# Transforms along w on quarters of the array, and a second spectral layer in groups of 192 channels

## The chip, the cores and the metric

The kernel runs on one core of a Trainium2 chip. The metric is the device time of one execution in microseconds (us), measured beside other executions of the same program; the median of three is given. One further execution was taken with the hardware profiler, and all rows shown are of that one. The engines are named as in the profile: PE is TensorE's matmul, PEld its weight load, DVE is VectorE, ACT is ScalarE, POOL is GpSimd, SP is SyncE, which issues most DMAs.

## The reference

Four layers run one after the other on an image of 48 x 48 positions with 768 channels, all in fp32. Layer 0 is an attention block with an MLP, layer 2 a scan of twelve steps with a 3x3 convolution. Layers 1 and 3 are the spectral layers, and they are what the change is about:

```python
bias = x
xs = jnp.fft.rfft2(xf32, axes=(1, 2))                     # along h and w, 48 x 25 modes
xs = xs.reshape(B, H, Wm, NUM_HEADS, BLOCK)               # 8 blocks of 96 channels
o1r = relu(einsum(xr, w1[0]) - einsum(xi, w1[1]) + b1[0]) # complex two-layer MLP per block
o1i = relu(einsum(xi, w1[0]) + einsum(xr, w1[1]) + b1[1])
o2r = einsum(o1r, w2[0]) - einsum(o1i, w2[1]) + b2[0]
o2i = einsum(o1i, w2[0]) + einsum(o1r, w2[1]) + b2[1]
out_c = softshrink(zr, LAMBDA) + 1j * softshrink(zi, LAMBDA)
out = jnp.fft.irfft2(out_c, s=(H, W), axes=(1, 2))
return out + bias
```

The transforms are linear, so the residual `bias` can be added to the image after the way back, or to the spectrum along w before the last step back.

## The kernel before

The transform over the image is done as matmuls with small constant matrices, in two steps: along w (48 positions to 25 modes with a real and an imaginary part) and along h.

*Forward along w, `spectrum_rows` (L1493).* A block is one of six groups `g` of eight image rows, and one `half` of the channels (384). The tile x has 96 partitions, two image rows side by side, and four such pairs. Four matmuls with a block-diagonal matrix `fw2` of 96 x 112 (two copies of the 48 to 50 transform, interleaved) each stream 384 columns (L1501). `Evac` copies the four results in turn on ACT and DVE to `ys`, and one DMA on SP stores it to `yu[half]` in DRAM, which has 112 rows, 24 pairs of image rows and 384 channels.

In the first spectral layer these blocks are called by `afno_follow` (L1642) from the MLP phase, where they stand among the MLP's matmuls: the MLP's second layer (L1029) stores a part of the image, `follow` loads it as `f1_x`, and a later call does the block. Their PSUM places come from the MLP's pool `ml_t` of two places (L909), which the transposes of the MLP use too; the MLP's products use another pool, `ml_m`, of six. The last of the twelve blocks is done at the start of `afno_first`. In the second spectral layer `rows_in` calls them between the matmuls of the scan's output (L1371), whose results get their bias on DVE (L1373), into a temporary tile, and Silu on ACT (L1374), into `x3`, a tile that holds the whole image with 96 partitions.

*The items, `spectrum_mix` (L1536).* For each half of the channels and each of five groups `kc` of five modes, the spectrum is loaded (`f_yt`, L1530), and four items, one for each block of 96 channels, are worked: transform along h (`f_x`, L1565), MLP (L1579 to L1581, L1600, L1601), softshrink on DVE, and back along h (`f_u`, L1615). The 40 items of a layer run as a pipeline of four stages. The result `f_us` goes back to `yu`. In the first layer (`keep` true) DVE adds the result to the loaded spectrum (L1618), so that the residual is in the spectrum; in the second layer `Evac` only copies.

*Back along w.* In the first layer `back` in `afno_first` (L1697) has the spectrum `f_gt` stationary (L1702). In the second layer `back` in `afno_second` (L1792 to L1804) takes a block of `yu` that is loaded ahead (`f_gt`, L1790, 100 of 112 rows used), does four matmuls with the block-diagonal `iw` of 100 x 96 (L1798), adds the result to `x3` on DVE (L1800), and issues the store on ACT's queue. The six blocks of the first half of the channels stand among the items of the second half; the six of the second half come behind all items, and their loads wait for the stores of the last items. For these the rows of the first four `kc` are loaded ahead (`most`) and the remaining rows last (`rest`).

A scheduler of the language orders the instructions of each engine from their dependences, and places of a pool are given out in turn. [...]

## Time and profile before

| what | value |
|---|---|
| median of three runs | 3671.11 us (3670.99 to 3674.01) |
| profiled execution, its own time | 3666.73 us |
| its span, first to last instruction | 3664.9 us |
| mean granted TensorE clock | 0.987 |
| MLP phase, with the first layer's rows in it | about 1660 to 2685 us |
| items of the first spectral layer | about 2685 to 2872 us |
| scan output with the second layer's rows | about 3320 to 3428 us |
| items of the second spectral layer | about 3428 to 3634 us |

Columns of the groups: line, engine, operation, out<-in, partitions x columns of the array with the shape, count, then busy time in us and mean ns of one, then idle time of the engine before them and what ended it. A record of a matmul lasts longer than its share of the array, as matmuls are pipelined; what counts is the time from one start to the next. Columns of the stretches: from and to, length, busy time (and count) of PE, PEld, DVE, ACT and POOL, granted TensorE clock, share of the DMA engines, GB/s. Columns of the timeline: start, duration, engine, line, operation, out<-in, shape, count of merged instructions, and in brackets idle time before.

### The profile page before, as it was taken

To read this page: it belongs to the slowest core of one execution; us is meant where nothing else is said; L and a number is where in the kernel's file an instruction comes from. 1 tells how busy PE (TensorE), PEld (TensorE's weight loads), DVE (VectorE), ACT (ScalarE), POOL (GpSimd) and SP (SyncE) were. 2 spreads that over 40 slices of the span, in tenths; PEclk is the share of its full clock that TensorE was granted. 3 is DMA by queue.
4 is the path that set the end of the run, shared out by engine and by line. 5 is a ranking of instruction groups with operands and counts; after the bars stand their busy time and mean duration, and the time that the engine had idled before them with its cause. 6 is when DMAs were issued, how large, how long until landed. Compare 5 with 4: busy or idle time off the path is not lost.

```text
span 3664.9 us, 52305 instructions
## 1 busy us (share of the span) xinstructions
PE 3567.0 (97%) x20914; PEld 2157.0 (59%) x20914; DVE 1998.1 (55%) x3011; ACT 1138.9 (31%) x1731; POOL 702.3 (19%) x570
## 2 busy tenths in 40 slices
PE   7999989999999999999999999999999998999998
PEld 4666544444444444455555555555578867995685
DVE  6644356667666666655324323332345578994455
ACT  1222244444444444303201210121023365223341
POOL 4211101111111111151000000000023303971131
PEclk9999989999999999999999999999999999999999
DMA  7666665646454443344345333533444302113345
GB/s 256 227 223 202 205 198 151 180 139 165 134 144 134 117 122 105 97 136 158 102 129 177 119 106 122 166 106 109 152 131 112 99 20 103 36 30 85 101 119 155
DMA packets 267739, 491.83 MB, mean 134 GB/s; under 512 B 37182, under 2 KB 220286, under 8 KB 261280
## 3 DMA queue, kind: packets, MB, share of 16 engines
q1 hardware_dynamic: 257680, 467.45, 42.9%
q10 hardware_dynamic: 9808, 20.94, 1.6%
q8 instruction: 168, 2.75, 0.3%
q14 instruction: 83, 0.68, 0.1%
HBM read 344.69 MB, written 143.62 MB: 133 GB/s over the span
## 4 chain that ended last, share of the span: by engine, by line
PE 82%; DMA 2%; DVE 2%; ACT 1%; issue 1%; POOL 1%; SPq 0%; DVEq 0%; ACTq 0%; POOLq 0%
PE p L966 13%; PE p L1029 13%; PE s L629 12%; PE av L660 12%; PE c L1286 6%; PE c L1193 4%; PE s L639 3%; PE pj L169 2%; PE f_z L1600 2%; PE f_z L1601 2%; PE f_x L1565 2%; PE so L1371 2%; PE f_u L1615 2%; PE f_w L1798 1%; PE f_o L1579 1%; PE f_o L1580 1%
## 5 line engine op out<-in xcount | busy, mean ns | idle before, releaser
L649 DVE TENSOR_TENSOR acc<-acc,p 128x928 f32<-128x928 f32 (+1 forms) x480 | 567.9, 1183 | 253.3 <-ACT p L641 220.6
L641 ACT ACTIVATE p<-s 128x928 f32<-128x928 f32 (+1 forms) x540 | 506.1, 939 | 524.4 <-PE s L639 496.3
L629 PE MATMUL s<-qt,kv 64*128 64x464 f32 (+1 forms) x2160 | 529.5, 566 | 3.0 <-DMA bt<-rw_d 3.0
L1029 PE MATMUL p<-w,h 128*128 128x384 f32 x1512 | 492.7, 486 | 0.0
L660 PE MATMUL av<-p,kv 128*64 128x464 f32 (+1 forms) x2160 | 457.3, 558 | 0.1
L1029 PEld LDWEIGHTS p<-w,h 128*128 128x128 f32 x1512 | 286.2, 190 | 196.9
L639 PE MATMUL s<-bt,oneh 64*128 64x464 f32 (+1 forms) x1080 | 399.3, 729 | 1.0 <-DMA bt<-rh_d 0.9
L629 PEld LDWEIGHTS s<-qt,kv 64*128 64x128 f32 x2160 | 195.4, 187 | 206.1 <-issue 199.8
L660 PEld LDWEIGHTS av<-p,kv 128*64 128x64 f32 x2160 | 142.2, 137 | 261.1 <-issue 257.1
L966 PE MATMUL p<-x2nT,w 128*128 128x384 f32 x864 | 292.7, 488 | 2.8 <-issue 2.8
L355 PE MATMUL qk<-xnT,wqk 128*128 128x384 f32 x756 | 253.5, 492 | 9.2 <-DMA wqk<-wqk_d 9.2
L1286 PE MATMUL c<-H,bands 128*48 128x96 f32 x5632 | 243.9, 247 | 11.4 <-issue 11.2
L1286 PEld LDWEIGHTS c<-H,bands 128*48 128x48 f32 x5632 | 234.4, 123 | 21.1 <-issue 11.5
L966 PEld LDWEIGHTS p<-x2nT,w 128*128 128x128 f32 x864 | 164.9, 191 | 118.3 <-issue 4.6
L966 PE MATMUL p<-xT,w 128*128 128x384 f32 x648 | 220.8, 486 | 0.0
L1005 POOL TENSOR_TENSOR rr<-rr,ml_b 128x1152 f32<-128x1152 f32 x12 | 32.2, 2684 | 952.9 <-DMA rr<-xr_d 885.2
L355 PEld LDWEIGHTS qk<-xnT,wqk 128*128 128x128 f32 x756 | 143.2, 193 | 104.3 <-issue 10.7
L961 ACT ACTIVATE h<-h,ml_b 128x384 f32<-128x384 f32 x144 | 88.3, 615 | 345.8 <-DVE h L981 174.3
L1294 POOL TENSOR_TENSOR t<-s,c 128x768 f32<-128x768 f32 x80 | 144.6, 1829 | 179.7 <-DMA bands<-in_bands_dram 168.4
L966 PEld LDWEIGHTS p<-xT,w 128*128 128x128 f32 x648 | 123.1, 190 | 85.8
L639 PEld LDWEIGHTS s<-bt,oneh 64*128 64x128 f32 x1080 | 106.4, 188 | 106.5 <-issue 102.3
L1600 PE MATMUL f_z<-f_w,f_o 97*96 97x96 f32 x800 | 134.4, 250 | 0.0
(324 smaller groups left out, 4666.7 us busy)
## 6 DMA issues: line engine op xcount, KB each, us to landing
w<-w1s_d SPq DMA_DIRECT2D x36, 768.0 KB, 4.1
w<-w2s_d SPq DMA_DIRECT2D x36, 768.0 KB, 4.3
w<-w1s_d SPq DMA_DIRECT2D x36, 576.0 KB, 3.6
w<-in_mlp_w_dram SPq DMA_DIRECT2D x27, 768.0 KB, 4.5
wqk<-wqk_d SPq DMA_DIRECT2D x12, 1344.0 KB, 6.9
yu<-f_ys SPq DMA_DIRECT2D x24, 672.0 KB, 3.8
f_yt<-yu SPq DMA_DIRECT2D x20, 720.0 KB, 6.5
yu<-f_us SPq DMA_DIRECT2D x18, 720.0 KB, 4.5
```

The lines of the kernel that those rows point to most:

```text
L355: nc.tensor.matmul(p[:, :TB], lhsT=w[:, n, c, :], rhs=ops[sb][n][:, c, :], start=c == 0, stop=c == NC2 - 1)
L629: nc.tensor.matmul(ps[:, s, :n], lhsT=keys[pr % 2][rows, kt * P : (kt + 1) * P], rhs=held(c)[rows, :n], start=True, stop=False)
L639: nc.tensor.matmul(ps[:, s, :n], lhsT=oneh[rows, b % 2, :], rhs=bts[b // 2][rows, j, :n], start=False, stop=True)
L641: nc.scalar.activation(p, ps[:, :, :n], AF.Exp)
L649: nc.vector.tensor_tensor(probs[c], probs[c], p, ALU.add)
L660: nc.tensor.matmul(avs[c][rows, : size(c)], lhsT=vals[pr % 2][:, kt, rows], rhs=p[:, s, :], start=kt == 0, stop=kt == NT - 1)
L966: nc.tensor.matmul(p[:, :TB], lhsT=w[n][:, c, :], rhs=rhs[n][:, c, :], start=c == 0, stop=c == NC2 - 1)
L1029: nc.tensor.matmul(ps[t][:, :TB], lhsT=hs[left, f][:, t * P : (t + 1) * P], rhs=wt[:, f % KW2, :], start=f == 0, stop=f == NF2 - 1)
L1193: nc.tensor.matmul(ps[:K, i, :n], lhsT=v[:, c, tok : tok + K], rhs=w[:, cc, c0 : c0 + n], start=cc == NC - 1, stop=cc == 0)
L1286: nc.tensor.matmul(ps[r0 : r0 + G, k // 4, cols], lhsT=bands[:, n - GC, i, :] if gr else bands0[:, n, i, :], rhs=H[:, n, :, d : d + NPR], ...
L1294: GP.tensor_tensor(t, sc[:, ch], c1[:, m0 : m0 + GC].unsqueeze(2).to_broadcast([P, GC, RR, NPR]), ALU.mult)
L1600: nc.tensor.matmul(out, lhsT=o1[:, j, 1:3, :].rearrange("c r h -> c (r h)"), rhs=w2t[:, b, 0, :], start=True, stop=False)
```

## The change

1. *Rows along w as quarters.* x and `x3` now have the second image row of a pair at partition 64 (112 partitions with a gap). The matrix `fw` is 48 x 64 (50 modes and zeros) and is loaded twice, at partitions 0 and 64. A block is eight matmuls of 64 output columns that stream 384 channels each: row half `a` of the array takes one image row of the pairs, column half `b` one pair of two, and the two row halves write to two PSUM banks. `yu[half]` becomes 64 x 48 x 384, one image row at a time, and a block is stored by two DMAs.
2. *Four PSUM places in the MLP.* The blocks take two places from `ml_t`, then two from `ml_m`, in turn.
3. *Items by groups.* `spectrum_mix` takes a list of groups of channels. The first layer keeps two groups of four blocks; the second has four groups of two blocks (192 channels), and five places instead of three for the loaded spectrum.
4. *Residual in the spectrum in both layers*, so the way back of the second layer copies (ACT and DVE in turn) instead of adding.
5. *Way back of the second layer.* Three blocks of sixteen image rows by 192 channels for each group, eight matmuls on quarters each, with `iw` of 50 x 48 (padded to 64) at partitions 0 and 64. The nine blocks of the first three groups stand among the items, the three of the last group behind them. Stores are two DMAs (one for each image row of the pairs) with 192 channels.
6. *Way back of the first layer.* `iw2` has 128 rows in place of 100; the matmuls keep 96 columns.
7. The scan's output adds the bias into `x3` and does Silu in place, on 112 partitions.

```diff
+        places = itertools.cycle(((pt, "t"), (pt, "t"), (pm, "m"), (pm, "m")))
+
         def psum(name):
-            return pt.tile([P, 512], F32, tag="t", name=name)
+            pool, tag = next(places)
+            return pool.tile([P, 512], F32, tag=tag, name=name)
...
-                            nc.tensor.matmul(ps[:BS, :TB], lhsT=hTs[j, pr // 4][:, pr % 4].rearrange("p s w -> p (s w)"), rhs=wo[:, j, cols], start=j == 0, stop=j == 1)
-                        t_ = tp.tile([BS, TB], F32, tag="t", name=f"st_{pr}_{half}")
-                        V.tensor_tensor(t_, ps[:BS, :TB], bo[:, cols], ALU.add)
-                        nc.scalar.activation(x3[:, pr, cols], t_, AF.Silu)
+                            nc.tensor.matmul(ps[:K, :TB], lhsT=hTs[j, pr // 4][:, pr % 4], rhs=wo[:, j, cols], start=j == 0, stop=j == 1)
+                        V.tensor_tensor(x3[:, pr, cols], ps[:K, :TB], bo[:, cols], ALU.add)
+                        nc.scalar.activation(x3[:, pr, cols], x3[:, pr, cols], AF.Silu)
...
-    ys = pool.tile([YR, 4, TB], F32, tag="ys", name=f"{name}_ys_{half}_{g}", bufs=bufs)
-    for i in range(4):
-        ps = psum(f"f_{half}_{g}_{i}")
-        nc.tensor.matmul(ps[:YR, :TB], lhsT=fw, rhs=x[:, i, :], start=True, stop=True)
-        ev(ys[:, i, :], ps[:YR, :TB])
-    nc.sync.dma_start(yu[half][:, 4 * g : 4 * g + 4, :], ys)
+    ys = pool.tile([P, 2, 2, TB], F32, tag="ys", name=f"{name}_ys_{half}_{g}", bufs=bufs)
+    for j in range(2):
+        ps = [psum(f"f_{half}_{g}_{j}_{a}") for a in range(2)]
+        for a in range(2):
+            keep = slice(a * HD, a * HD + G)
+            for b in range(2):
+                nc.tensor.matmul(ps[a][b * HD : (b + 1) * HD, :TB], lhsT=fw[keep], rhs=x[keep, 2 * j + b, :], start=True, stop=True)
+        for a in range(2):
+            ev(ys[:, j, a, :], ps[a][:, :TB])
+    for b in range(2):
+        nc.sync.dma_start(pairs_of(yu[half], b, g), ys[b * HD : (b + 1) * HD].rearrange("p j a c -> p (j a) c"))
+
+def pairs_of(yu, b, g):
+    n = b * (G // 2) + 4 * g
+    return yu[:, n : n + 4, :]
...
-            if keep:
-                nc.vector.tensor_tensor(us[:, :, cols], pv, yt[:, :, cols], ALU.add)
-            else:
-                ev(us[:, :, cols], pv)
+            nc.vector.tensor_tensor(us[:, :, cols], pv, yt[:, :, cols], ALU.add)
...
-        items = [(half, kc, b) for half in halves for kc in range(NKC) for b in range(HB)]
+        items = [(g, kc, b) for g, (_, _, n) in enumerate(groups) for kc in range(NKC) for b in range(n)]
...
+        GB = 2
+        groups = [(n * GB // (NB // 2), n * GB % (NB // 2), GB) for n in range(NB // GB)]
...
-        def back(half, g):
-            cols = slice(half * TB, (half + 1) * TB)
-            gt = gts.pop((half, g))
-            last = half == 1 and g == NTB - 1
-            for i in range(4):
-                ps = psum(f"w_{half}_{g}_{i}")
-                nc.tensor.matmul(ps[:BS, :TB], lhsT=iw, rhs=gt[: 4 * KW, i, :], start=True, stop=True)
-                dst = x3[:, 4 * g + i, cols]
-                nc.vector.tensor_tensor(dst, ps[:BS, :TB], dst, ALU.add)
+        def store(queue, prs, cols):
+            for s in range(2):
+                queue.dma_start(out[s, :, prs, cols], x3[s * HD : s * HD + G, prs, cols])
+
+        def back(group, c):
+            cols = channels(group)[2]
+            gt = gts.pop((group, c)).rearrange("p (j s) c -> p s j c", s=2)
+            for j in range(2):
+                ps = [psum(f"w_{group}_{c}_{j}_{b}") for b in range(2)]
+                for b in range(2):
+                    keep = slice(b * HD, b * HD + KR)
+                    for s in range(2):
+                        nc.tensor.matmul(ps[b][s * HD : (s + 1) * HD, : 2 * W], lhsT=iw[keep], rhs=gt[keep, s, 2 * j : 2 * j + 2, :], start=True, stop=True)
+                for b in range(2):
+                    ev(x3p[:, b, 4 * c + 2 * j : 4 * c + 2 * j + 2, cols], ps[b][: HD + G, : 2 * W].rearrange("p (j c) -> p j c", j=2))
+                if group == len(groups) - 1:
+                    store((nc.scalar, nc.sync)[j], slice(8 * c + 4 * j, 8 * c + 4 * j + 4), cols)
+            if group < len(groups) - 1:
+                store(nc.scalar, slice(8 * c, 8 * c + 8), cols)
...
+        loads = {each * (q + 1) + 5 + 2 * c: (q, c) for q in range(final) for c in range(3)}
+        backs = {step + 2: at for step, at in loads.items()}
...
+            if step == each * len(groups) + 1:
+                for c in range(3):
+                    load(final, c, most)
```

## The prediction

> **What bounds the kernel now.** I read the page first: busy shares, slices and the chain that ended last.
>
> ```profile
> PE 3567.0 (97%) x20914; PEld 2157.0 (59%) x20914; DVE 1998.1 (55%) x3011; ACT 1138.9 (31%) x1731; POOL 702.3 (19%) x570
> PE 82%; DMA 2%; DVE 2%; ACT 1%; issue 1%; POOL 1%; SPq 0%; DVEq 0%; ACTq 0%; POOLq 0%
> ```
>
> TensorE is busy for 97% of the span and is 82% of the chain. So the change is worth the TensorE time that it takes out, plus what it does to the few places where TensorE waits. The groups by line and shape give the transforms along w, and two groups for comparison:
>
> ```profile
> L1286 PE MATMUL c<-H,bands 128*48 128x96 f32 x5632 | 243.9, 247 | 11.4 <-issue 11.2 <-DVE s L1306 0.3
> L1565 PE MATMUL f_x<-f_fh,f_yt 96*96 96x96 f32 x800 | 83.7, 253 | 2.4 <-DMA f_yt<-yu 1.2 <-issue 1.1
> L1501 PE MATMUL f_f<-f_x,f_fw 96*112 96x384 f32 x88 | 34.2, 497 | 0.0
> L1798 PE MATMUL f_w<-f_gt,f_iw 100*96 100x384 f32 x96 | 34.0, 508 | 8.9 <-DMA f_gt<-yu 8.9
> L1501 PE MATMUL so_f<-x,f_fw 96*112 96x384 f32 x96 | 32.9, 486 | 0.0
> ```
>
> An fp32 matmul of the program leaves two records; 96 of them are 48 matmuls. Both first rows stream 96 columns. L1565, over the whole array, costs 83.7/800 = 105 ns a record; L1286, which writes partitions 0-47 and 64-111 in turn, costs 243.9/5632 = 43 ns. So two column halves run at once. The timelines of the attention and of the row transforms show the same for row halves, and what a change of tiling costs:
>
> ```profile
> 902.82 2.56 PE L660 MATMUL av<-p,kv 128*64 128x464 f32 x12
> 905.31 1.05 PE L629 MATMUL s<-qt,kv 64*128 64x464 f32 x4
> ...
> 906.41 0.94 PE L629 MATMUL s<-qt,kv 64*128 64x464 f32 x4
> ...
> 907.39 0.95 PE L629 MATMUL s<-qt,kv 64*128 64x464 f32 x4
> ...
> 908.48 1.00 PE L668 MATMUL rs<-acc,ones 128*64 128x464 f32 x4
> 909.31 2.50 PE L660 MATMUL av<-p,kv 128*64 128x464 f32 x12
> 911.74 1.05 PE L629 MATMUL s<-qt,kv 64*128 64x464 f32 x4
> ```
>
> ```profile
> 3356.05 2.75 PE L1501 MATMUL so_f<-x,f_fw 96*112 96x384 f32 x8
> 3358.63 2.75 PE L1371 MATMUL so<-wo,hT 128*96 128x384 f32 x8
> ```
>
> Eight records of 384 columns take 3358.63 - 3356.05 = 2.58 us, 322 ns each, one after the other; 464 columns would take 389 ns. Twelve records of L660 take 911.74 - 909.31 = 2.43 us, which is six times 389 ns and 0.10: pairs. Last, the end, as stretches and as TensorE's timeline:
>
> ```profile
> 3430.00:3576.00 146.00, 143.79 (x1168) 121.75 (x1168) 69.41 (x139) 59.34 (x140) 45.94 (x63) 0.98 0.35 98
> 3576.00:3636.00 60.00, 57.45 (x393) 42.27 (x391) 35.20 (x68) 16.75 (x39) 12.51 (x17) 1.00 0.48 134
> 3640.00:3650.00 10.00, 7.66 (x19) 3.77 (x19) 4.32 (x8) 0.00 (x0) 0.00 (x0) 0.70 0.64 146
> 3650.00:3660.00 10.00, 9.84 (x31) 4.73 (x29) 8.54 (x17) 0.00 (x0) 0.00 (x0) 1.00 0.92 288
> ```
>
> ```profile
> 3632.48 0.97 PE L1615 MATMUL f_u<-f_Z,f_ih 96*96 96x480 f32 x2
> 3642.34 17.50 PE L1798 MATMUL f_w<-f_gt,f_iw 100*96 100x384 f32 x48 [8.89 <-DMA f_gt<-yu]
> ```
>
> The last spectral item leaves TensorE at 3633.45, the last spectrum goes out and comes back (8.89 us), half of the way back runs (17.5), and 5.1 us later the last store has landed: 31.4 us of tail.
>
> **The change, part by part.** Its sums are made against the profiled execution, 3666.73 us with a span of 3664.9; the median of the timed runs is 4.4 us above it, so I take the gain off the median.
>
> *Price of a quarter block.* A block is eight image rows by 384 channels. Before: four matmuls, eight records in series, 2.58 us. After: eight matmuls, sixteen records, each on one of four quarters (row half by column half), two PSUM banks for the two row halves. No row shows both halvings at once. From below: four records at once, 16/4 x 322 = 1.29 us. From above: two at once, as every row shows, 2.58 us. A gain beyond 1.29 is excluded, since a quarter streams its own 384 columns. I take four: the pairs of column halves share the moving rows and the pairs of row halves share the output partitions, and both run at the full rate, so neither side is the limit that a quarter would meet. To it comes the change of tiling, in and out. From the attention's rows: 0.10 at the end of L660 (2.43 against 2.33), 0.12 in the first L629 behind it (905.31 to 906.41 is 1.10, the next 0.98), 0.11 at the last one (907.39 to 908.48 is 1.09), 0.05 in L668 (0.83 against 0.78): 0.38 for both ways. Ends: nothing, or double, 0.76, as an untiled neighbour is not in any row. So a block costs 1.67 us.
>
> [...]
>
> *Rows of the first layer, inside the MLP.* Twelve blocks. Eleven stand among MLP matmuls and take 2.80 us now (2.11 to 2.16 for six records, then 0.65 for two that wait for a PSUM place); one takes 2.60 at the layer's start. 11 x (2.80 - 1.67) + (2.60 - 1.67) = 13.4 us gained. The two further places come out of the six of the MLP's products, so after such a block the next product's tiles wait for a place that the product just ended frees: a VectorE add of about 0.55 us against 0.65 us of the tile before it. Between nothing and 0.5 us each; I charge 1.0 in all. Twelve more store issues at 0.3 us on SP lie beside matmuls, as MLP weights land 4 us after issue and are prefetched; were that cover gone they would cost 3.6 us.
>
> *Rows of the second layer.* Twelve blocks of 2.58: 12 x 0.91 = 10.9 us gained. The cover for evacuation: per block four adds (554 ns) and two copies (557) on VectorE, 3.3 us, four Silu (522) and two copies (467) on ScalarE, 3.0 us, beside 5.2 + 1.7 us of TensorE. The wider output, 112 rows, costs nothing: those engines' times go by columns. The Silu in place adds no wait, as it already followed its add.
>
> *Way back inside the items.* Now six blocks of 2.58 = 15.5 us stand among the items. After: nine of 1.67 = 15.0. Gained 0.5. The residual moves into the spectrum's add, on VectorE, and the alternation with ScalarE goes. The first layer already has that add (653 ns, the copy is 654), and VectorE is busy 69.41 of 146 us here: nothing. The way back's copies leave VectorE half of the adds it had.
>
> *DMAs.* Rows of 384 channels become 192, so packets in this phase halve in size. If each took as long as before, the shares 0.35 and 0.48 would go to 0.70 and 0.96: still below full. On SP the loads for a group's way back stand behind the landing of that group's last spectrum store (4.5 us), and behind them the next store and the next spectrum loads. These loads are issued three items, 13.7 us, before use, against 6.5 to 7.6 us to land. A store on ScalarE's queue waits for VectorE's copy, as it now waits for the add.
>
> *Tail.* The wait of 8.89 stays: last store, landing, load. Then three blocks instead of six double ones: 24 matmuls on quarters, 12 x 322 = 3.9 us. The clock granted behind the wait was 0.70, and 48 records took 17.5 where 15.5 is full rate: another 2.0. Then copy 0.6 and landing 4.5. Together 8.9 + 5.9 + 0.6 + 4.5 = 19.9. The stores set a second bound: 1.77 MB at the 288 GB/s seen at the end is 6.1 us, from 1.6 us behind the wait, and 2 to land: 18.6. I take 19.9; gained 31.4 - 19.9 = 11.5, between 9 and 14.
>
> Sum: 13.4 - 1.0 + 10.9 + 0.5 + 11.5 = 35.3 us. 3671.1 - 35.3 = 3636 (the profiled execution would be 3631). Its own range: without the price of switching, 33 x 0.38 = 12.5 more, and a tail of 17.4: 3621; with double that price and a tail of 22.4: 3651.
>
> **The rivals.**
>
> *Two at once.* The quarters run only in pairs, as all rows show. A block is 2.58 + 0.38 = 2.96. First rows: 11 x (2.80 - 2.96) + (2.60 - 2.96) = -2.1, and -1.0; second rows 12 x -0.38 = -4.6; way back 15.5 - 9 x 2.96 = -11.1; tail 8.9 + 7.7 + 2.0 + 0.6 + 4.5 = 23.7, +7.7. Together 11.1 slower: 3682. For it: no row has four. Against it: nothing in the pairs is at a limit. It decides from 35.3/33 = 1.07 us more a block, 2.74 us, which is 2.2 records at once.
>
> *Three at once, on average.* 5.3 slots of 322: 0.43 more a block, 33 x 0.43 = 14.2, and 1.3 in the tail: 3651.
>
> *Late transfers.* Every one of the nine blocks inside the items waits, in order, for its load, 3 us each: 27 us back, 3663. For it: smaller packets, a queue that waits for landings. Against: 6 us of margin.
>
> *The tail does not shrink.* The stores crowd with the last loads (share 0.92 now) and the gain there is nil: 3648.
>
> **How the numbers follow.** Four at once 0.64, three 0.09, two 0.12, late transfers 0.06, tail 0.06, something not named 0.03 (slower). The forecast is 3636. The range 3620 to 3656 covers four, three and the tail, leaving out two at once and late transfers, 0.18. No change that a measurement can tell is within 0.2%, 7.3 us: above 3664 is reached by late transfers at their worst and by an overlap between two and three. Faster 0.82, same 0.05, slower 0.13.
>
> **What would show it.** Right: the records of a row block start in fours, a block leaves 1.6 to 1.8 us until the next matmul; three short blocks of about 6 us behind the last wait; no new idle time before the MLP's products. Wrong: records of a block starting in twos, idle time of TensorE on the spectrum's loads among the items, or a wait of the last blocks that is well above 9 us.

## The result, and the profile after

The changed kernel takes 3650.04 us (median of 4 runs, 3645.78 to 3651.64) against 3671.05 us for the kernel before (median of 4, 3668.43 to 3674.01): ratio 0.9941, 95% interval 0.9923 to 0.9958, 21.0 us less. The forecast was 35.3 us less, 3636. The sign is right and the time lies in the range, but only 60% of the gain came.

The profiled execution of the changed kernel took 3650.99 us, with a span of 3649.2. It lies 0.95 above its median, while the profiled execution of before lies 4.3 below its own; so the two profiles differ by only 15.7 us. Here is where these 15.7 us lie. Each stage runs from the start of its first matmul to the start of the next stage's first (the MLP and the second layer's items to the end of their last matmul, the tail from there to the end of the span).

| stage | before, us | after, us | difference | forecast |
|---|---|---|---|---|
| up to the MLP | 1666.5 | 1669.3 | +2.8 | 0 |
| MLP with the first layer's rows | 1015.7 | 1004.3 | -11.4 | -11.4 |
| MLP's end to the first layer's items | 1.2 | 1.7 | +0.5 | 0 |
| first layer's items and way back, start of the scan | 389.3 | 392.7 | +3.4 | -0.9 |
| the scan's steps | 246.3 | 246.4 | +0.1 | 0 |
| scan's output with the second layer's rows | 109.1 | 99.3 | -9.8 | -10.9 |
| second layer's items | 205.3 | 209.1 | +3.8 | -0.5 |
| tail | 31.5 | 26.5 | -5.0 | -11.5 |

Of the first row nothing is due to the change: in the twelve further kernels below, which all have the same code up to there, it lies between 1666.0 and 1671.3, 1668.4 in the mean. The profile of before had a fast start, and that is 1.9 of its 4.3 us.

The page of the changed kernel, its busy times and the engines of the chain:

```profile
PE 3537.7 (97%) x21202; PEld 2132.3 (58%) x21202; DVE 2000.3 (55%) x3007; ACT 1142.7 (31%) x1735; POOL 705.1 (19%) x570
...
PE 75%; DVE 5%; ACT 2%; DMA 2%; issue 1%; POOL 1%; ACTq 0%; SPq 0%; DVEq 0%; POOLq 0%
```

TensorE is still busy for 97%. Its part of the chain went from 82 to 75%, and those of DVE and ACT from 2 to 5% and from 1 to 2%. The page puts that on lines of the scan's steps (L1309, L1293 and L1298), where the change did nothing and the time is the same, so it is no sign of the change. The groups of TensorE by line and shape (busy us, mean ns; idle time before):

```profile
L1590 PE MATMUL f_x<-f_fh,f_yt 96*96 96x96 f32 x800 | 84.1, 254 | 3.5 <-issue 1.8 <-DMA f_yt<-yu 1.7
...
L1838 PE MATMUL f_w<-f_gt,iw 50*64 50x384 f32 x192 | 20.6, 548 | 13.0 <-DMA f_gt<-yu 13.0
...
L1514 PE MATMUL so_f<-x,fw 48*64 48x384 f32 x192 | 18.9, 496 | 0.0
L1514 PE MATMUL f_f<-f_x,fw 48*64 48x384 f32 x176 | 16.7, 495 | 0.0
```

The rows of the second layer (so_f) went from 32.9 us with 96 records to 18.9 with 192. A single record still lasts 496 ns, as before (486): they overlap. The timeline of TensorE inside the MLP shows one block between its neighbours:

```profile
2029.62 2.10 PE L969 MATMUL p<-xT,w 128*128 128x384 f32 x6
2031.65 1.52 PE L1514 MATMUL f_f<-f_x,fw 48*64 48x384 f32 x16
2033.10 4.14 PE L969 MATMUL p<-x2nT,w 128*128 128x384 f32 x12
```

From 2031.65 to 2033.10 are 1.45 us for sixteen records. In 23 of the 24 blocks they start at 0, 0.006, 0.013 and 0.020 us, then at 0.373 to 0.393, 0.696 to 0.716, and 1.018 to 1.038: four at once, and from the second four on 322 ns apart. Only the last block of the second layer is drawn out, to 1.66 us for its last start. Last, the tail, as timeline of all engines (SPq and ACTq are the DMA issues of SyncE and ScalarE):

```profile
3619.17 5.41 SPq L1824 DMA_DIRECT2D f_gt<-yu  x6
...
3622.78 0.65 DVE L1643 TENSOR_TENSOR f_us<-f_u,f_yt 96x480 f32<-96x480 f32 x1 [1.14 <-PE f_u L1641]
3624.71 2.94 SPq L1647 DMA_DIRECT2D yu<-f_us  x2
3633.15 2.19 SPq L1824 DMA_DIRECT2D f_gt<-yu  x6
3635.79 6.88 PE L1838 MATMUL f_w<-f_gt,iw 50*64 50x384 f32 x48 [13.05 <-DMA f_gt<-yu]
...
3642.90 1.02 ACTq L1828 DMA_DIRECT2D out_dram<-x  x2
3643.96 0.48 ACT L63 COPY x<-f_w 112x384 f32<-112x384 f32 x1 [1.09 <-issue]
```

The wait ahead of the last blocks is 13.05 us, where it was 8.89. Read the first three lines together: the data of the last spectrum store was ready at 3622.78 + 0.65 = 3623.43, but SyncE was issuing the six early loads (`most`) from 3619.17 to 3624.58, and the two last stores stand behind them on its queue; the second of these was issued from 3626.16 to 3627.65. These issues took up to 1.6 us each, where the six late loads, from 3633.15 on, took 0.28 to 0.34 us each. The first early load waited for the store ahead of them, of the fourth fifth of the spectrum, which was issued at 3615.04 and landed at 3619.17. At the end ScalarE's last copy stands behind ScalarE's own store issues. The stretches of the tail (PE, PEld, DVE, ACT and POOL busy, then granted TensorE clock, DMA share, GB/s):

```profile
3624.00:3634.00 10.00, 0.00 (x0) 0.00 (x0) 0.00 (x0) 0.00 (x0) 0.00 (x0) 0.50 0.51 148
3634.00:3644.00 10.00, 6.88 (x48) 3.26 (x48) 3.35 (x6) 2.34 (x6) 0.00 (x0) 0.66 0.60 137
```

The clock was granted at one half from 3623.8 for 17.07 us.

### The profile page after: what moved, and what is told of

Read it like the earlier page. It is cut to its first block, busy times and chain, and to the rows that moved or that the text cites. A ratio compares the mean times of both kernels' runs of the same rounds, so it can differ in the third digit from the quotient of the medians.

```text
span 3649.2 us, 52995 instructions
## 1 busy us (share of the span) xinstructions
PE 3537.7 (97%) x21202; PEld 2132.3 (58%) x21202; DVE 2000.3 (55%) x3007; ACT 1142.7 (31%) x1735; POOL 705.1 (19%) x570
## 4 chain that ended last, share of the span: by engine, by line
PE 75%; DVE 5%; ACT 2%; DMA 2%; issue 1%; POOL 1%; ACTq 0%; SPq 0%; DVEq 0%; POOLq 0%
PE p L969 13%; PE p L1032 13%; PE s L629 12%; PE av L660 12%; PE c L1196 4%; PE s L639 3%; PE pj L169 2%; PE f_x L1590 2%; DVE s L1309 2%; PE f_z L1625 2%; PE f_z L1626 2%; PE so L1374 2%; PE f_u L1641 2%; DVE H L1293 2%; ACT c L1298 2%
## 5 line engine op out<-in xcount | busy, mean ns | idle before, releaser
L1289 PE MATMUL c<-H,bands 128*48 128x96 f32 x5632 | 243.6, 247 | 11.5 <-DVE th L1227 10.9
```

The lines of the kernel that those rows point to most:

```text
L1289: nc.tensor.matmul(ps[r0 : r0 + G, k // 4, cols], lhsT=bands[:, n - GC, i, :] if gr else bands0[:, n, i, :], rhs=H[:, n, :, d : d + NPR], ...
```

## The experiments

The theory after this reading: the quarters do what was forecast, and the missing 14 us are in how the pieces meet: SyncE's order in the tail, bytes in flight there, the drain and the start of the second layer's items, a changed order at the start of the scan, and half clock behind TensorE's pauses. The rival: the quarters themselves, the PSUM places or the regrouping brought less than their share. All kernels are edits of the changed one. Times, each with the ratio to the kernel before in the same session:

| run | us, median | ratio, 95% interval | wait of the last blocks | tail |
|---|---|---|---|---|
| e1_most_act | 3648.36 | 0.9935 (0.9919 to 0.9952) | 10.48 | 23.2 |
| e2_pair_order | 3650.76 | 0.9941 (0.9925 to 0.9958) | 13.20 | 26.5 |
| e3_two_places | 3666.94 | 0.9985 (0.9976 to 0.9995) | 12.60 | 25.9 |
| e4_groups_384 | 3656.00 | 0.9957 (0.9943 to 0.9971) | 8.49, then 6.55 | 35.7 |
| e5_early_rows | 3641.99 | 0.9917 (0.9901 to 0.9934) | 5.96 | 19.3 |
| e6_drain_backs | 3648.74 | 0.9938 (0.9921 to 0.9954) | 14.20 | 27.5 |
| e7_scan_order | 3646.17 | 0.9934 (0.9918 to 0.9951) | 11.07 | 24.2 |
| e8_warm | 3649.34 | 0.9938 (0.9922 to 0.9955) | 12.01 | 24.5 |
| e9_warm_start | 3648.75 | 0.9931 (0.9915 to 0.9946) | 13.88 | 27.3 |
| e10_tail | 3642.38 | 0.9917 (0.9904 to 0.9931) | 8.74 | 22.1 |
| e11_tail_start | 3643.23 | 0.9916 (0.9903 to 0.9930) | 6.73 | 18.8 |
| e12_both_starts | 3636.42 | 0.9904 (0.9888 to 0.9919) | 6.48 | 19.3 |

The wait is from the last matmul of the items to the first of the last blocks (in e8, e10, e11 and e12 unread matmuls stand in it). The changed kernel and e2, e3, e7 and e9 have the same code in the tail, and their waits run from 11.07 to 13.88: a difference of 2 us in the wait or in a median is not a verdict, and the stages below are judged by their own times.

### e1_most_act: the early loads leave SyncE's queue

```diff
-        def load(group, c, rows=slice(0, KR)):
+        def load(group, c, rows=slice(0, KR), queue=nc.sync):
...
-                nc.sync.dma_start(gts[group, c][b * HD
+                queue.dma_start(gts[group, c][b * HD
...
-                    load(final, c, most)
+                    load(final, c, most, nc.scalar)
```

> The six early loads of the last group's spectrum are issued by ScalarE's queue instead of SyncE's; nothing else changes. My theory of the tail: the two last spectrum stores stood behind these six issues on SyncE (3619.17 to 3624.58), although the data of the last one was ready at 3623.43, so it left 4.2 us too late. Then SyncE issues the last store within 0.5 us of its data, TensorE's wait ahead of the last blocks falls from 13.05 to about 9 us and the kernel is 4 us faster than the changed one: about 3646. The rival, that the wait is the store's own landing and the way back (which my forecast took as 8.89) lengthened by the narrower rows: the wait stays within 1 us of 13 and the time at 3650.

The timeline of its tail:

```profile
3620.95 6.54 ACTq L1824 DMA_DIRECT2D f_gt<-yu  x5
...
3623.48 0.65 DVE L1643 TENSOR_TENSOR f_us<-f_u,f_yt 96x480 f32<-96x480 f32 x1 [1.14 <-PE f_u L1641]
3628.62 5.94 SPq L1824 DMA_DIRECT2D f_gt<-yu  x6
3633.93 6.24 PE L1838 MATMUL f_w<-f_gt,iw 50*64 50x384 f32 x48 [10.48 <-DMA f_gt<-yu]
```

The last store was issued at 3624.16, with its data (3624.13), and seen landed at 3628.62, 5.2 us behind the end of the items in place of 10.4. So the queue's order did cost what was claimed, 5 us. But from there to the first matmul it now took 5.3 us, where it was 2.6 (3633.15 to 3635.79): the early loads, issued up to 3627.5, were still moving, at 195 to 218 GB/s in the stretches from 3624 to 3632, and the late loads came behind them. Half was given back, and the wait of 10.48 is near the lowest of the unedited tail, 11.07. The expectation of 9 us missed for that reason. In this run 5 us were saved in issue and order, and 2.7 lost to bytes.

### e2_pair_order: the same quarters in another order

```diff
-    for j in range(2):
-        ps = [psum(f"f_{half}_{g}_{j}_{a}") for a in range(2)]
-        for a in range(2):
-            keep = slice(a * HD, a * HD + G)
+    for a in range(2):
+        ps = [psum(f"f_{half}_{g}_{j}_{a}") for j in range(2)]
+        keep = slice(a * HD, a * HD + G)
+        for j in range(2):
             for b in range(2):
```

> Both row transforms into the spectrum (24 blocks) issue the same eight quarter matmuls in another order: the four of one row half first, then the four of the other. My theory: matmuls run at once only as long as neighbours in the program's order use different quarters, so now two run at once (the two column halves) and a block takes 8 x 322 = 2.58 us and some 0.35 for the change of tiling, 1.29 more than now; 24 x 1.29 = 31 us slower than the changed kernel, about 3681, above the kernel before. The rival: TensorE looks far enough ahead to find a free quarter whatever the order, the records still start in fours, and the time stays at 3650. Anything between (some overlap across the border between the two row halves) gives a block between 1.65 and 2.9 us.

The theory fell; the rival has it. The same place in the MLP:

```profile
2028.70 1.53 PE L1514 MATMUL f_f<-f_x,fw 48*64 48x384 f32 x16
2030.16 4.14 PE L969 MATMUL p<-x2nT,w 128*128 128x384 f32 x12
```

1.46 us, where 2.93 was expected. The records start at 0, 0.007, 0.027 and 0.033 us, then at 0.374 to 0.406. By the program's order the first two take the two quarters of one row half; the next two are read as those of the other, whose first record stands eight records later in the program, since records on the same quarters start 322 ns apart in the changed kernel. The scheduler could have changed the order of the instructions instead; VectorE's copies speak against that (first line the changed kernel, second e2):

```profile
2032.62 1.20 DVE L65 COPY f_ys<-f_f 128x384 f32<-128x384 f32 x2
2030.26 1.02 DVE L65 COPY f_ys<-f_f 128x384 f32<-128x384 f32 x2 [0.53 <-PE f_f L1514]
```

VectorE's first copy belongs to the second product in the program's order. It starts 0.97 us into the block in the changed kernel, and 1.56 us into it, after a wait, in e2. TensorE's signals for the four products come at 0.89, 0.95, 1.53 and 1.59 us in the changed kernel, and at 0.89, 1.53, 1.59 and 1.65 us in e2. So in e2, by this reading, the third product ran beside the first, and its signal, at 1.59, came behind that of the second, at 1.53: the signals kept the written order, and the starts of the matmuls did not. That a matmul started early because its quarter was free is the author's inference. So the gain is in the quarters and does not hang on the order in which they are written.

### e3_two_places: two PSUM places in the MLP

```diff
-        places = itertools.cycle(((pt, "t"), (pt, "t"), (pm, "m"), (pm, "m")))
+        places = itertools.cycle(((pt, "t"),))
```

> The row blocks inside the MLP use the two PSUM places they had before, in place of four; the rest of the change stays. My theory: the second half of a block must wait until the first half's two copies (about 0.5 us each) have freed the places, and the scheduler fills that with a tile of the MLP, so each of eleven blocks pays 0.5 to 1.3 us in idle time or a further change of tiling: 6 to 14 us slower than the changed kernel, 3656 to 3664. The rival, that the places bought nothing and the whole gain of the MLP's blocks is from the quarters: 3650, and the MLP phase stays at 1003.8 us.

The MLP takes 1027.6 us: 23.3 more than with four places, more than expected, and 11.9 more than the kernel before, which had two places and no quarters. The timeline of one block, and the wait of the group:

```profile
2035.56 0.88 PE L1514 MATMUL f_f<-f_x,fw 48*64 48x384 f32 x8
2037.00 0.86 PE L1514 MATMUL f_f<-f_x,fw 48*64 48x384 f32 x4 [0.57 <-ACT f_ys L63]
2037.79 0.91 PE L969 MATMUL p<-x2nT,w 128*128 128x384 f32 x2
2038.63 0.86 PE L1514 MATMUL f_f<-f_x,fw 48*64 48x384 f32 x4
2039.42 3.49 PE L969 MATMUL p<-x2nT,w 128*128 128x384 f32 x10
```

```profile
PE f_f L1514 <- ACT f_ys L63: 6.6, 11, 0.6
```

The block falls into three pieces: it waits 0.57 us for a copy, the second half runs in pairs instead of fours, and a tile of the MLP stands between, with a further change of tiling. From 2035.56 to 2039.42, less the 0.65 us of the MLP's own tile, are 3.2 us in place of 1.45; eleven blocks make 19. Two stretches of half clock of 3.41 us, at 1997.7 and 2342.4, which the changed kernel has not, make up to 3.4 more. The other stages of this profile together took 6.5 us less than in the changed kernel's, and the median is 16.9 us above it. Quarters without the places lose; the gain of the MLP belongs to both together.

### e4_groups_384: the second layer in two groups again

The core of the edit; the way back takes four pairs by 384 channels at a time, six times for each group.

```diff
-        GB = 2
+        GB = 4
...
-        loads = {each * (q + 1) + 5 + 2 * c: (q, c) for q in range(final) for c in range(3)}
+        loads = {each * (q + 1) + 5 + 2 * c: (q, c) for q in range(final) for c in range(NTB)}
...
-                for c in range(3):
+                for c in range(NTB - 1):
                     load(final, c, most)
```

> The second spectral layer works again in two groups of 384 channels in place of four of 192; quarters, residual in the spectrum and all else of the change stay. Inside the items stand six blocks of the way back in place of nine: 3 x 1.63 = 4.9 us less. Behind the last spectrum stand six blocks in place of three: 3.9 us more at full clock, up to 7.7 at half clock. By the terms of my forecast that is all, with the wait as it is: 3.9 - 4.9 + some 2 for the clock = +1, 3651. By my theory of the tail ten early loads (in place of six) now stand ahead of the last stores on SyncE, at 0.9 us each: the wait grows from 13 to about 17 us, and with the slower clock behind a longer wait the time is 3655 to 3660.

6 us slower than the changed kernel, in the expected 3655 to 3660, but by another way. The items took 205.2 us, 3.9 less, of the 4.9 expected for three blocks fewer. The last stores were on time here, since the early loads had started sooner. The tail is 9.2 us longer:

```profile
3630.14 8.63 PE L1838 MATMUL f_w<-f_gt,iw 50*64 50x384 f32 x64 [8.49 <-DMA f_gt<-yu]
...
3638.92 1.96 PE L1838 MATMUL f_w<-f_gt,iw 50*64 50x384 f32 x16 [0.15 <-ACT x L63]
...
3647.43 4.21 PE L1838 MATMUL f_w<-f_gt,iw 50*64 50x384 f32 x16 [6.55 <-DMA f_gt<-yu]
```

Twice the blocks stand there, and the sixth waits 6.55 us for its load, which gets a place only when the first block is done and was issued at 3641.30, among the output's stores. So the groups of 192 channels are worth some 6 us against this layout of 384 with five places for `f_gt`; whether a sixth place would take the wait of 6.55 us away was not tested.

### e5_early_rows: less left to load behind the last store

```diff
-        most, rest = slice(0, 2 * KC * (NKC - 1)), slice(2 * KC * (NKC - 1), KR)
+        most, rest = slice(0, 2 * KC * (NKC - 2)), slice(2 * KC * (NKC - 2), KR)
...
-            if step == each * len(groups) + 1:
+            if step == each * len(groups):
```

> On the changed kernel, the early loads of the last group fetch three fifths of the spectrum's rows, one step sooner, and the loads behind the last store fetch two fifths in place of one. So nothing stands on SyncE ahead of the two last spectrum stores, and the 1.44 MB that the early loads moved at some 215 GB/s in the tail (6.7 us, as the run with these loads on ScalarE showed: their transfers lay ahead of the last loads) are mostly through before. My theory, that the tail is set by queue order and by bytes in flight: last store issued with its data, landed 4.5 us later, the first two late loads (240 KB) 3 us later, TensorE's wait 8.5 to 9.5 us in place of 13.05, time about 3646. The rival, that the time of landing is fixed by the late loads whatever stood ahead: they now carry twice the bytes, and the wait is 11 to 13, time 3649 to 3650.

The theory is confirmed, and by more than expected:

```profile
3605.96 2.69 SPq L1824 DMA_DIRECT2D f_gt<-yu  x6
...
3613.42 8.72 SPq L1647 DMA_DIRECT2D yu<-f_us  x3
...
3624.41 2.29 SPq L1824 DMA_DIRECT2D f_gt<-yu  x6
3627.08 6.81 PE L1838 MATMUL f_w<-f_gt,iw 50*64 50x384 f32 x48 [5.96 <-issue]
```

The six early issues take 2.69 us in place of 5.41. The last store, issued at 3621.84, was seen landed at 3624.41, after 2.57 us, where it took 7.0 in the changed kernel and 4.5 in e1 (a store of twice the bytes took 5.1 in the kernel before). The late loads, with twice the bytes, took 2.67 us, as in the changed kernel (2.64). The wait is 5.96 us, the tail 19.3, and the time 3641.99 us: 8.0 us below the changed kernel, with runs (3640.48 to 3643.6) that don't meet its runs. This is the part of the missing gain that two lines of the change had cost. The early loads now need three fifths of the spectrum and no longer wait for the store of the fourth; whether the earlier step alone would do was not tested.

### e6_drain_backs: work for the drain of the items

```diff
-        backs = {step + 2: at for step, at in loads.items()}
+        backs = {step + 2 if at[0] < final - 1 else each * len(groups) + at[1]: at for step, at in loads.items()}
```

> On the changed kernel, the three blocks of the way back of the third group stand in the last three steps of the items (as three did in the kernel before) instead of two, four and six steps ahead of the end. My theory: the 3.8 us that the items lost are partly the idle time of the pipeline's drain (waits of 0.31 and 1.43 us on VectorE's Z, and pitches of 6.11, 4.27, 4.24, 4.15), which these blocks then fill; the items end 1.5 to 2.5 us sooner and the time is 3648. The rival: the last item's Z is what the end waits for, the blocks delay it or their copies stand ahead of it on VectorE, and nothing is gained: 3650 or up to 2 us more.

The items took 205.6 us, 3.5 less, and no wait on f_Z is left: the drain was idle, and the blocks fill it. (1.4 of the 3.5 are at the start, where the half clock was 10.24 us long in this run and 13.65 in the other, so the drain gave 2.1.) The waits on f_Z in the changed kernel, as total, count and longest:

```profile
PE f_u L1641 <- DVE f_Z L1631: 1.7, 2, 1.4
```

But the wait of the last blocks grew:

```profile
3616.60 1.02 PE L1641 MATMUL f_u<-f_Z,f_ih 96*96 96x480 f32 x2
3631.82 6.62 PE L1838 MATMUL f_w<-f_gt,iw 50*64 50x384 f32 x48 [14.20 <-DMA f_gt<-yu]
```

The data of the last store was ready at 3618.31, but the six early loads stood on SyncE from 3616.18 to 3620.88, and the store was issued at 3621.99 and landed 7.2 us later. The early loads had waited for the store of the fourth fifth, which took 6.3 us to land in place of 4.1. That the output's stores of the moved blocks, issued at 3608.90, 3613.22 and 3617.46, made these landings longer is likely and not shown. By the median 1.3 us are left, which is within the noise. Both expectations are met in part: the items gain, the end does not.

### e7_scan_order: TensorE's old order at the start of the scan

```diff
+                first = rows_back.heads[0, 0, 0].ins
...
+                                with tc.issue_after(first) if q == 0 else ExitStack():
                                     nc.tensor.matmul(ps[:K, i, :n], lhsT=v[:, c, tok : tok + K], rhs=w[:, cc, c0 : c0 + n], start=cc == NC - 1, stop=cc == 0)
```

Here `heads` keeps the last matmul of the first piece of the way back, and the scan's first products are ordered behind it.

> On the changed kernel, TensorE's order at the start of the scan is put back to that of the kernel before: the first block of the first layer's way back stands ahead of the scan's first products, instead of behind five of them. My theory: the wait of 2.01 us on VectorE's memset of the first PSUM tile and the 3.41 us of half clock behind it were a matter of that order; the stretch from the way back's first matmul to the first matmul of the scan's steps is 2 to 2.6 us shorter, time about 3648. The rival: the memset is late for any order, since VectorE reaches it only behind the last copy of the way back, and TensorE waits elsewhere: no change.

The rival has it. TensorE's waits name the same memset, at another matmul (first fence the changed kernel, second e7):

```profile
PE c L1196 <- DVE c L1149: 2.0, 1, 2.0
```

```profile
PE c L1728 <- DVE c L1149: 1.9, 1, 1.9
```

From the way back's first matmul to the scan's first step it took 203.2 us, where the changed kernel took 203.4 and the kernel before 200.7. The median of 3646.17 is then not from this edit; its profile has the shortest wait of the unedited tails, 11.07. In e1, e6 and e12, which keep the order of the changed kernel, the same stretch took 201.6, each time without the half clock of 3.41 us at its start. So 1.7 of the 2.7 us are the clock; why the memset ends later than before stays open.

### e8_warm: TensorE kept busy in the wait

```diff
+        for n in range(15):
+            nc.tensor.matmul(psum(f"warm_{n}")[:BS, :CH], lhsT=opened[0][0], rhs=x3[:BS, 0, :CH], start=True, stop=True)
         for c in range(3):
             load(final, c, rest)
```

> On the changed kernel, 15 matmuls of 480 columns whose results nobody reads (12.2 us at full clock) fill TensorE's wait ahead of the last blocks. My theory: the half clock in the tail (17.07 us from 3623.8) follows from TensorE's idle time; without idle time it stays away, the last three blocks take 4.2 us in place of 6.88, and the time is 2 to 3 us shorter, 3647 to 3648. The rival: the half clock comes whatever TensorE does at the end of the items, the idle matmuls then run at half rate, take up to 24 us, and push the last blocks back: 3650 to 3660.

The stretches of the unread matmuls and of the last blocks:

```profile
3623.20:3635.40 12.20, 12.20 (x31) 4.73 (x30) 0.65 (x1) 0.00 (x0) 0.00 (x0) 1.00 0.63 168
3635.40:3640.00 4.60, 4.10 (x49) 1.84 (x48) 3.19 (x6) 1.34 (x3) 0.00 (x0) 1.00 0.50 107
```

The clock is whole, 1.00 where the changed kernel had 0.50 and 0.66, and the last blocks take 4.10 us in place of 6.88: with TensorE's wait filled, the half clock of this tail stayed away. But from the last matmul to the end it now took 8.4 us (6.5 before): the end waits for the stores. 1.9 us of tail gained by the profiles, 0.7 by the medians.

### e9_warm_start: no pauses at the start of the items

```diff
+        def idle(n):
+            for i in range(n):
+                m = nc.tensor.matmul(psum("idle")[:BS, :CH], lhsT=opened[0][0], rhs=x3[:BS, 0, :CH], start=True, stop=True)
+                tc.keep_in_program_order(m)
+
         def beside(step):
+            if step < 2:
+                idle(2)
```

> On the changed kernel, two matmuls of 480 columns that nobody reads stand behind each of the first two items' transforms of the second layer, where TensorE waits 1.45 and 1.43 us for POOL's sum. My theory, from the run that filled the tail's wait: the half clock of 13.65 us at 3415.6 answers TensorE's pauses at the start of the items; with one pause of the three left (1.8 us ahead of the first item) the half clock is gone or a few us long, and the stretch from the first item's transform to the first inverse transform, 17.7 us, is 13 to 15 us: time 3645 to 3647. The rival: the half clock answers the pause ahead of the items or the change of work, comes as before, and the idle matmuls at half rate (1.6 us each) add 2 to 3 us: 3652.

The stretch from the first item's transform to the first inverse transform, of the changed kernel and of this one:

```profile
3413.65:3431.31 17.66, 14.78 (x78) 12.74 (x79) 4.43 (x11) 4.64 (x11) 3.65 (x5) 0.61 0.18 45
```

```profile
3415.80:3429.41 13.61, 12.57 (x86) 9.29 (x87) 4.48 (x11) 4.41 (x11) 3.62 (x5) 1.00 0.24 59
```

TensorE does four more matmuls and is 4.05 us faster, since the clock is 1.00 in place of 0.61. The items took 205.0 us in place of 209.1. By the medians 1.3 us are left: this profile's wait in the unedited tail is 13.88, and the time up to its items is 2.2 us longer.

### e10_tail, e11_tail_start, e12_both_starts: the parts together

e10 takes the edits of e5 and e6, seven unread matmuls in the tail's wait, and this order in the last block:

```diff
-                if group == len(groups) - 1:
+                if group == len(groups) - 1 and c < 2:
                     store((nc.scalar, nc.sync)[j], slice(8 * c + 4 * j, 8 * c + 4 * j + 4), cols)
+            if group == len(groups) - 1 and c == 2:
+                for j in range(2):
+                    store((nc.scalar, nc.sync)[j], slice(8 * c + 4 * j, 8 * c + 4 * j + 4), cols)
```

> On the changed kernel, together: the early loads of three fifths of the rows one step sooner (8.0 us in its own run), the third group's way back in the drain (1.3), seven unread matmuls in the tail's wait (in their own run the last blocks took 4.10 us in place of 6.88), and in the last block both halves' copies ahead of their stores, so that ScalarE's last copy does not stand behind ScalarE's store issues (1.1 us). My theory: the parts act at different places and add, 8.0 + 1.3 + 2.5 + 1.0 = 12.8: 3637. The rival: what comes sooner only waits for the bytes of the stores at the end (1.77 MB at 290 GB/s is 6.1 us from the first copy on), so only the first part counts: 3641 to 3642.

The rival has it: the time is that of e5 alone. The items end sooner, at 205.5 us, but the last store, issued at 3617.56 right behind the stores of the blocks in the drain, was seen landed at 3622.62, after 5.06 us in place of 2.57. What the drain gave, the store took. The last blocks took 7.45 us: the seven matmuls end 3.1 us too soon, and the half clock came all the same (6.83 us from 3624.8).

e11 leaves the drain as it was, and adds the edit of e9:

> On the changed kernel, together, and without the blocks in the drain: the early loads of three fifths of the rows one step sooner (8.0 us in its own run), both halves' copies ahead of their stores in the last block, seven unread matmuls in the tail's wait, and two unread matmuls behind each of the first two items' transforms of the second layer (in their own run the stretch to the first inverse transform took 13.6 us in place of 17.7). My theory: the start and the tail do not touch, so 8.0 + 4.1 and 1 to 3 for the clock in the tail: 3635 to 3637. The rival, from the run with blocks in the drain: what comes sooner meets more bytes in flight, the last store lands later (5.05 us there, 2.57 without), and the time is 3639 to 3642.

3643.23 us, no better than e5, and so above both expectations. The tail is the shortest of all, 18.8 us, but the start took 15.2 us in place of e9's 13.6, with a half clock of 3.41 us at 3416.3, and another one, at 3621.1, fell on the last item. With the same two unread matmuls a half clock came at the start here and none in e9 (clock 1.00).

e12 adds seven unread matmuls at the first layer's start:

```diff
             last = 2 * NKC * (NB // 2)
+            for i in range((2, 5)[step] if step < 2 else 0):
+                m = nc.tensor.matmul(psum("idle")[:BS, :CH], lhsT=opened[0][0], rhs=opened[0][1].rearrange("c b r o -> c (b r o)")[:, :CH], start=True, stop=True)
+                tc.keep_in_program_order(m)
```

> The same, and seven unread matmuls at the start of the first spectral layer's items: two behind the first item's transform and five behind the second's, where TensorE waits 1.45 and 4.17 us for POOL (the second POOL sum stands behind two memsets). My theory: these pauses bring the half clock of 13.65 us there too; without it, the stretch from the first layer's first transform to its first inverse transform, 19.4 us, is 14 to 16, and the time is 3 to 5 us below the kernel without this part. The rival: the pause ahead of the items (1.7 to 2.5 us) is enough for the half clock here, the unread matmuls then run at half rate and cost 2 to 4 us.

As expected here: 15.4 us from the first transform to the first inverse one, in place of 19.4, and no half clock from 1675 to 3054. The stage from the first transform to the scan's steps is 387.3 us in place of 392.7, which takes back the 3.4 us lost to the kernel before. The time is 3636.42 us (3634.88 to 3640.54), 6.8 below e11 and 13.6 below the changed kernel, with an interval of the ratio (0.9888 to 0.9919) that ends below the changed kernel's (0.9923): it beats both kernels. Of the 6.8, 5.7 lie in this stage. Some of the rest is luck: the second layer's start, with the same code as e11, took 13.6 us in place of 15.2. The unread matmuls of its tail, and its last blocks:

```profile
3615.29 6.76 PE L1876 MATMUL f_warm<-x,f_fh 96*96 96x480 f32 x14
3621.98 4.99 PE L1841 MATMUL f_w<-f_gt,iw 50*64 50x384 f32 x48
```

## Why the prediction was right, and where it was not

*The price of a quarter block: right.* Forecast 1.29 + 0.38 = 1.67 us. Measured are 1.45 from the block's start to the next matmul, 0.09 by which the record ahead of the block takes longer than usual, and 0.10 on the neighbour's second record: 1.645, of which 0.35 is the change of tiling in and out. The choice of the attention's rows as the nearest for that price held, though their neighbours are tiled as well. The rivals of two and of three at once fall with the starts of the records, and e2 shows four at once in another order as well. Sixteen records of 322 ns took 1.29 us here, 4.0 times, on two by two halves.

*Rows inside the MLP: right, with two errors that cancel.* The MLP gained 11.4 us, as forecast. The charge of 1.0 for the PSUM places was not needed: no product waits for a place. But the half clock at the MLP's start reached 5.5 us into it, in place of 3.2, and took back about as much: half of the 2.3 us, an estimate. That the places are a condition of the gain and not a cost was not seen: without them the MLP is 23.3 us slower (e3).

*Rows of the second layer: right but for the last block.* 9.8 of 10.9 us. The twelfth block gave nothing: the items' start behind it waits for evacuation, 3.9 us from its start to the first transform, as before. The 112 rows of the scan's output cost next to nothing: its add took 558 ns on 112 rows and 554 on 96, its Silu 524 and 522.

*Way back inside the items: the term was wrong by 4.3 us.* "Gained 0.5" counted blocks, nine of 1.67 against six of 2.58, and that price held: an item with a block takes 1.63 us more than one without. It left out where they stood. Before, three of the six lay in the drain of the pipeline, the last steps, where no new item begins; after the change one of nine does, and TensorE waits there 1.7 us for f_Z (e6: two blocks more in the drain, 2.1 us). And the half clock at the start was 13.65 us in place of two times 3.41: the stretch to the first inverse transform took 17.7 us, and 15.5 before, which is another 2.1 (e9: 13.6 without the pauses).

*Tail: the step that failed is "the wait of 8.89 stays".* It measured 13.05, and a wait well above 9 us was one of the signs that I had named for being wrong. I had listed SyncE's queue among those that the moved loads pass, for the items, and found margin there; for the tail, where the six early loads stand directly ahead of the two stores that end the wait, I did not read the queue. e1 shows that order: without it the store landed 5.2 us sooner behind the end of the items, and 2.7 of these were lost again to the bytes in flight. Two further terms were too small: the last blocks took 6.88 for 5.9, behind a half clock of 17.07 us, and from the last matmul to the end 6.5 for 5.1, as the last copy stands behind ScalarE's issues. With the queue and the bytes out of the way (e5) the tail is 19.3 us, against a forecast of 19.9. The late transfers among the items did not come: items without a block keep their 4.57 us.

The result of 3650.04 also fits two rivals by number, three at once (3651) and a tail that does not shrink (3648). Neither happened: a time near a rival's is no evidence for it while its rows say otherwise.

*Not in the sum:* 3.4 us lost between the first layer's first transform and the scan's steps, where 0.9 were to be gained. 2.7 lie at the start of the scan (e7). The other 0.7 are the rest of 2.5 us lost at the start of the first layer's items, which took 19.4 us in place of 16.8: in the new order of POOL the second sum stands directly behind the memsets (4.2 us of wait, 2.4 before), and 13.65 us of half clock lie there, from 2678.3, of which e12 has none. In e3, where POOL does the memsets right behind the first sum, the longest wait is 1.5 us and the same stretch takes 16.3. The change does not move these instructions in its text; the scheduler laid both places out anew.

## What to carry to other kernels

Where a change moves DMAs, write down each queue as a list around every wait that ends the path, with the time at which each entry can start: here the price of the moved loads was the entry behind them, 5 us in the tail, and the bytes in flight, 2.7 us (e1). The edit that saved matmul time was worth its price only with the PSUM places: the MLP took 11.4 us less than before with four, and 11.9 more with two (e3). Blocks that filled the idle drain of the pipeline cost less there than among the items: two more of them in the drain gained 2.1 us, of 3.3 at the full price (e6). Judge parts by their own stage in the profile: here the same code in one stage took up to 5.3 us more in one kernel's profile than in another's, as much as a part is worth.

## What the runs showed of the hardware that was not expected

In e2 the records of a block started at 0, 0.007, 0.027 and 0.033 us, the third of them read as one that stands eight records behind the first in the program, while the signals of the four products came in the program's order, at 0.89, 1.53, 1.59 and 1.65 us.

In the profiles of both kernels the half clock comes in pieces of 3.41 us. Each has thirteen stretches, whose starts lie whole multiples of 3.4133 us apart, within 0.003 us: in the changed kernel 3060.6, 3316.6, 3415.6 and 3623.8 are 75, 29 and 61 pieces apart. The lengths are one to five pieces, but for the last of each profile, at the end of the span (3.91 us before, 6.92 after). In the changed kernel pauses of 1.8, 1.45 and 1.43 us within 10 us stand with 13.65 us of half clock; with the latter two filled it was gone in e9, and one piece of it was left in e11. In the kernel before, pauses of 1.14, 1.45 and 1.55 us at the same place stand with two single pieces. What decides between these was not shown by a run.

In the tail of the changed kernel an issue of a DMA on SyncE took from 0.28 to 1.6 us. The last spectrum store, of 180 KB, landed 2.57 us after its issue began in e5, while the DMA engines moved 81 GB/s, and 4.5 (e1), 5.1 (e10), 7.0 (changed kernel) and 7.2 us (e6) after it where they moved 147 to 195 GB/s.
